# Ten products of the identity ahead of the first data, and a new order of the first loads, in a two-layer mixture and adapter kernel

## The chip, the cores and the metric

The kernel runs on one NeuronCore of a Trainium2 chip. The metric is device time in microseconds (us), the median of several runs. The engines are named as in the profile: PE is TensorE (the matmul array) and PEld its weight loads, DVE is VectorE, ACT is ScalarE, POOL is GpSimd, and SP is SyncE, which here only issues DMA transfers (loads and stores). "SPq" and "ACTq" are the instruction queues from which those engines issue transfers.

## The reference

The input `x` has 8 sequences of 256 tokens with 1024 features. Two residual layers follow. The first is a dense product with a mixture of low-rank experts, the second a dense product with one weight matrix per sequence, chosen by an id:

```python
base = jnp.einsum('btd,od->bto', x, W)
logits = jnp.einsum('btd,ed->bte', x, Wr) + one_hot(language_ids, 8)[:, None, :] * 5.0
topw, topi = jax.lax.top_k(logits, 2)
weights = jax.nn.softmax(topw, axis=-1)
gates = jnp.sum(one_hot(topi, 8) * weights[..., None], axis=-2)
h = jnp.einsum('btd,erd->bter', x, A)                  # 8 experts of rank 16
lora_out = jnp.einsum('bter,bte,eor->bto', h, gates, B)
x = x + base + 2.0 * lora_out
x = x + jnp.einsum('bsi,boi->bso', x, weight[adapter_ids])
```

`W`, and each `weight[i]`, is 1024 by 1024. `A` gives 128 columns per feature and `Wr` gives 8. All numbers are float32.

## The kernel before, in words

The host lays out `x` as blocks: `xT[i, j, c]` is feature half `i`, token half `j` (1024 tokens) and half `c` of that token half (512 tokens). Such a chunk holds four pieces `k` of 128 features by 512 tokens, 256 KB each. The blocks live in SBUF as `xb["11"]` to `xb["22"]`, where the profile calls them `x`. `A` and `Wr`, transposed and joined, are `aw_sb`: for each of the eight 128-feature pieces, 136 columns, 68 KB. It lies in the memory of a `y` block, so the profile calls it `y`.

The head of the kernel issues all loads of the first layer. `load_x` (line 104) and `load_w` (line 109) issue from SyncE. `load_aw` (line 112) issues from ScalarE in three pieces, of two, two and four feature pieces (lines 115, 118 and 119). The language and adapter ids, 8 integers each, copied to all 128 partitions, follow on ScalarE (lines 122 and 123). On SyncE come the four 256 KB pieces of `xT[0, 0, 0]` one by one (line 117), the two 512 KB halves of `xT[1, 0, 0]` (lines 120 and 121), and then whole 1 MB chunks of x, the four blocks of W and B.

The tile framework gives each load one of eight DMA semaphores in turn, counted over both issuing engines, so that a load waits at its issue until the load eight before it has landed. The order of loads in the source is therefore also the order of these waits.

GpSimd meanwhile makes `ident`, a 128 by 128 identity matrix, and two small index tables.

From line 510 on, the order of instructions is the one written out by hand. `use_ids()` (line 151) turns the ids into a bias table and adapter numbers, in small VectorE operations. `project(j, c)` (line 186) computes `h` and the logits for 512 tokens: for each of eight feature pieces and four groups of 128 tokens it multiplies an x tile (128 by 128, the weights of the array) with a piece of `aw_sb` (136 columns), adding up in the PSUM tile `ps_h`. So the first quarter, `project(0, 0)`, needs all of `aw_sb` and the chunks `xT[0, 0, 0]` and `xT[1, 0, 0]`; `project(0, 1)` needs `xT[0, 0, 1]` and `xT[1, 0, 1]`, and so on for the four quarters. After each quarter VectorE adds the bias and writes the logits `lg`, and ScalarE copies `h` out. `gating(j)` turns logits into gates for a token half, and `turn(j)` transposes the gated `h` with products of `ident` into `ps_g`.

Then come the seven products of a Strassen scheme for the first layer (`product`, line 356; PSUM tiles A, B and X at line 366), with sums and differences of blocks made by VectorE between them, and 16 groups of the second layer (`adapter_group`, line 462; products at line 474), each half of the output columns of one sequence. The adapter weights are loaded by SyncE from `load_w1` (line 417), three groups ahead. All PSUM tiles come from one pool of four (`bank`, line 87) and go round in order.

Of the kernel before, what the change touches and what calls it, by code (L numbers as in the profile page):

```python
# [16 lines left out]
P = 128  # L17
NE = 8
LANG_BIAS = 5.0
SCALING = 2.0  # L20
NEG = -3.0e38


@with_exitstack
def kernel(
# [25 lines left out]
    nc = tc.nc  # L51
# [9 lines left out]
    KH = KC // 2  # L61
# [22 lines left out]
    def flat(blk):  # L84
        return blk.rearrange("p k n -> p (k n)")

    def bank(name):
        return psum.tile([P, 2, TQ], F32, name=name, tag="acc")
# [10 lines left out]
    aw_sb = flat(yb["12"])[:, : KC * EA].rearrange("p (k e) -> p k e", k=KC)  # L99
    hT = [flat(yb["22"])[:, j * C * ER : (j + 1) * C * ER].rearrange("p (c e) -> p c e", c=C) for j in range(2)]  # L100
    b_sb = const.tile([ER, O], F32, name="b_sb")
    ids = const.tile([P, 2, NB], I32, name="ids")

    def load_x(queue, i, j, c, k0, k1):
        queue.dma_start(  # L105
            xb[f"{i+1}{j+1}"][:, k0:k1, c * TQ : (c + 1) * TQ], xT[i, j, c, :, k0:k1, :]
        )
# [1 line left out]
    def load_w(i, j):  # L109
        nc.sync.dma_start(wb[f"{i+1}{j+1}"], wT[i, j])  # L110

    def load_aw(k0, k1):
        nc.scalar.dma_start(aw_sb[:, k0:k1, :], awT[:, k0:k1, :])  # L113

    load_aw(0, 2)
    for k in range(KH):
        load_x(nc.sync, 0, 0, 0, k, k + 1)
    load_aw(2, 4)
    load_aw(4, 8)
    load_x(nc.sync, 1, 0, 0, 0, 2)  # L120
    load_x(nc.sync, 1, 0, 0, 2, 4)
    nc.scalar.dma_start(ids[:, 0, :], lang.partition_broadcast(P))
    nc.scalar.dma_start(ids[:, 1, :], adapt.partition_broadcast(P))
    load_x(nc.sync, 0, 0, 1, 0, 4)
    load_x(nc.sync, 1, 0, 1, 0, 4)
    load_x(nc.sync, 0, 1, 0, 0, 4)
# [10 lines left out]
    ident = const.tile([P, P], F32, name="ident")  # L137
# [13 lines left out]
    def use_ids():  # L151
        nc.vector.tensor_copy(ids_f, ids)

        nc.vector.tensor_tensor(
            bias,
            ids_f[:, 0, :].unsqueeze(2).to_broadcast([P, NB, E]),
            ecol.unsqueeze(1).to_broadcast([P, NB, E]),
            ALU.is_equal,
        )
        nc.vector.tensor_scalar(bias, bias, LANG_BIAS, None, ALU.mult)  # L160

        wrap = const.tile([P, NB], F32, name="wrap")
        nc.vector.tensor_scalar(wrap, ids_f[:, 1, :], 0.0, float(NAD), ALU.is_lt, ALU.mult)
        nc.vector.tensor_tensor(wrap, ids_f[:, 1, :], wrap, ALU.add)
        nc.vector.tensor_scalar(aid_i, wrap, 0.0, float(NAD - 1), ALU.max, ALU.min)
# [20 lines left out]
    def project(j, c):  # L186

        ps = bank(f"ps_h_{j}_{c}")
        for k in range(KC):
            for r in range(CQ):  # L190
                v, u = divmod(r, 2)
                nc.tensor.matmul(  # L192
                    ps[:, v, u * EA : (u + 1) * EA],
                    lhsT=xk(k, j, c)[:, ts(r, P)],
                    rhs=aw_sb[:, k, :],
                    start=(k == 0 and u == 0),
                    stop=(k == KC - 1),
                    skip_group_check=True,
                )
        ps = ps[:, :, : 2 * EA].rearrange("p v (u e) -> p v u e", u=2)  # L200
        split = lambda t: t[:, c * CQ : (c + 1) * CQ, :].rearrange("p (v u) e -> p v u e", v=2)
        nb = CQ * P // S
        b0 = (2 * j + c) * nb
        add(
            split(lg[j]),
            ps[:, :, :, ER:],
            bias[:, b0 : b0 + nb, :].unsqueeze(2).to_broadcast([P, nb, CQ // nb, E]),
        )
        nc.scalar.copy(split(hT[j]), ps[:, :, :, :ER])
# [16 lines left out]
    def gating(j):  # L226
# [11 lines left out]
        def onto_h():  # L238
# [5 lines left out]
        ops = ops1 + [  # L244
            lambda: nc.vector.scalar_tensor_tensor(rest, hot1, NEG, lg[j], ALU.mult, ALU.add)
        ] + ops2 + [
# [261 lines left out]


    ctx.enter_context(tc.manual_schedule())  # L510
    use_ids()
    project(0, 0)
    project(0, 1)
# [104 lines left out]
```

## Time and profile before

| what | us |
|---|---|
| median of 3 runs (lowest to highest) | 434.15 (434.06 to 434.67) |
| the profiled execution | 434.59 |
| its span, from first to last instruction | 432.8 |
| PE busy in the span | 422.8 |
| DVE busy in the span | 273.7 |
| first product of `project` starts at | 5.35 |
| last product of `project` ends at about | 38.5 |

The profile is of one execution; times in it count from the start of the span. A line of a group or a wait names the source line, the engine, the operation and the tiles, `out<-in`. A wait is put down to what ended it. A stage table gives, for a stretch of time, the busy time of each engine with the number of its instructions, the granted clock of TensorE, the mean busy share of the core's 16 DMA engines, and the GB/s that they moved. A float32 product shows as two records of PE.

### The profile page before, as it was taken

The page shows a single profiled execution, that of the slowest core. Times are in us where ns is not written, and L with a number is a line of the kernel's source. Part 1 is how long each engine was busy: PE and PEld are TensorE (multiplying, and loading weights), DVE is VectorE, ACT ScalarE, POOL GpSimd, SP SyncE. Part 2 cuts the span into 40 slices and gives each one's busy share as a digit, 9 for nine tenths or more (in the row PEclk, how much of TensorE's full clock was granted, in tenths as well). Part 3 has the DMA queues.
Part 4 walks back from the last instruction along what each step waited for, and adds up shares of the span by engine and source line. Part 5 has one row for each costly group of instructions (what it writes and reads, how often), then busy time and mean ns, then how long its engine had stood idle before and what let it go on. Part 6 is the DMA issues. An engine that isn't in the chain of part 4 may idle for free.

```text
span 432.8 us, 4177 instructions
## 1 busy us (share of the span) xinstructions
PE 422.8 (98%) x1624; PEld 289.8 (67%) x1624; DVE 273.7 (63%) x347; ACT 37.8 (9%) x81; POOL 0.9 (0%) x8
## 2 busy tenths in 40 slices
PE   5899999999999999999999999999999999999996
PEld 4897444444444444444445888888888888888885
DVE  1058696744538887999864756666776656666631
ACT  1011210002000000000000111111111111111110
POOL 0000000000000000000000000000000000000000
PEclk9999999999999999999999999999999999999999
DMA  7996000000002020045000056655555555665211
GB/s 221 391 402 253 0 0 2 0 0 0 2 0 97 8 89 0 2 165 220 3 0 0 26 220 243 242 228 192 192 195 221 219 231 224 243 242 203 89 48 50
DMA packets 14963, 55.88 MB, mean 129 GB/s; under 512 B 1632, under 2 KB 1888, under 8 KB 10336
## 3 DMA queue, kind: packets, MB, share of 16 engines
q1 hardware_dynamic: 14224, 55.06, 33.8%
q10 hardware_dynamic: 720, 0.57, 0.4%
q8 instruction: 13, 0.21, 0.2%
q14 instruction: 6, 0.05, 0.0%
HBM read 47.23 MB, written 8.39 MB: 128 GB/s over the span
## 4 chain that ended last, share of the span: by engine, by line
PE 96%; DMA 3%; ACTq 0%; SPq 0%; ACT 0%; issue 0%
PE A L474 26%; PE A L366 24%; PE B L366 14%; PE B L474 13%; PE X L366 7%; PE X L474 6%; PE ps_h L192 5%; DMA x<-xT_dram 2%; DMA y<-awT_dram 1%; PE ps_g L263 0%; ACTq L113 0%; SPq L105 0%; ACT w L352 0%; ACTq L352 0%
## 5 line engine op out<-in xcount | busy, mean ns | idle before, releaser
L366 PE MATMUL A<-t,s 128*128 128x512 f32 x112 | 50.4, 592 | 0.0
L474 PE MATMUL B<-x,w 128*128 128x256 f32 x192 | 45.4, 379 | 0.0
L168 DVE TENSOR_TENSOR w<-X,w 128x256 f32<-128x256 f32 x16 | 6.8, 425 | 59.9 <-PE X L474 59.9
L474 PE MATMUL A<-x,y 128*128 128x256 f32 x192 | 44.2, 379 | 0.0
L352 ACT COPY w<-A 128x256 f32<-128x256 f32 x48 | 17.9, 372 | 257.2 <-PE A L474 257.2
L474 PEld LDWEIGHTS A<-x,y 128*128 128x128 f32 x192 | 36.5, 190 | 5.4 <-issue 0.5
L474 PEld LDWEIGHTS B<-x,w 128*128 128x128 f32 x192 | 36.5, 190 | 5.0
L168 DVE TENSOR_TENSOR x<-x 128x1024 f32<-128x1024 f32 x32 | 39.1, 1222 | 0.8
L366 PEld LDWEIGHTS A<-t,s 128*128 128x128 f32 x112 | 21.3, 190 | 26.8 <-issue 26.8
L192 PE MATMUL ps_h<-y,x 128*128 128x136 f32 x256 | 32.0, 288 | 6.5 <-DMA y<-awT_dram 5.3
L168 DVE TENSOR_TENSOR y<-A,y 128x1024 f32<-128x1024 f32 x22 | 26.8, 1220 | 17.3 <-PE A L366 17.3
L192 PEld LDWEIGHTS ps_h<-y,x 128*128 128x128 f32 x256 | 31.3, 198 | 6.9 <-DMA y<-awT_dram 5.3
L474 PE MATMUL X<-x,y 128*128 128x256 f32 x128 | 30.2, 379 | 0.0
L168 DVE TENSOR_TENSOR x<-x,x 128x1024 f32<-128x1024 f32 x24 | 28.6, 1216 | 0.0
L474 PEld LDWEIGHTS X<-x,y 128*128 128x128 f32 x128 | 24.3, 190 | 3.3
L366 PE MATMUL A<-x,w 128*128 128x512 f32 x56 | 25.2, 592 | 0.0
L366 PE MATMUL B<-t,s 128*128 128x512 f32 x56 | 25.2, 592 | 0.0
L366 PE MATMUL X<-x,w 128*128 128x512 f32 x56 | 25.2, 592 | 0.0
L366 PE MATMUL B<-x,s 128*128 128x512 f32 x56 | 25.2, 592 | 0.0
L366 PE MATMUL A<-t,w 128*128 128x512 f32 x56 | 25.2, 592 | 0.0
L168 DVE TENSOR_TENSOR y<-B,y 128x1024 f32<-128x1024 f32 x12 | 14.6, 1221 | 16.2 <-PE B L366 16.2
L474 PE MATMUL A<-w,w 128*128 128x256 f32 x96 | 22.7, 379 | 0.0
(92 smaller groups left out, 433.5 us busy)
## 6 DMA issues: line engine op xcount, KB each, us to landing
x<-w_dram SPq DMA_DIRECT2D x32, 1024.0 KB, 5.0
out_dram<-w SPq DMA_DIRECT2D x32, 256.0 KB, 2.0
x<-xT_dram SPq DMA_DIRECT2D x6, 1024.0 KB, 13.3
w<-wT_dram SPq DMA_DIRECT2D x4, 1024.0 KB, 14.4
x<-xT_dram SPq DMA_DIRECT2D x4, 256.0 KB, 4.6
x<-xT_dram SPq DMA_DIRECT2D x2, 512.0 KB, 6.6
b_sb<-bT_dram SPq DMA_DIRECT2D x1, 512.0 KB, 14.7
y<-awT_dram ACTq DMA_DIRECT2D x2, 136.0 KB, 4.8
```

Of the source, the lines that this page charges most:

```text
L168: nc.vector.tensor_tensor(out_, x, y, op)
L192: nc.tensor.matmul(ps[:, v, u * EA : (u + 1) * EA], lhsT=xk(k, j, c)[:, ts(r, P)], rhs=aw_sb[:, k, :], start=(k == 0 and u == 0), stop=(k ...
L352: nc.scalar.copy(dest, acc)
L366: nc.tensor.matmul(acc[:, m, :], lhsT=l, rhs=r, start=(first and i < 2), stop=(i >= len(steps) - 2), skip_group_check=True,)
L474: nc.tensor.matmul(acc[name], lhsT=lhs[:, k // 2, k % 2, :], rhs=rhs[:, k, :], start=(first and k == 0), stop=(k == KH - 1), skip_group_ch ...
```

## The change

Three things change in the head, and nothing after it.

First, a PSUM tile `idle` is taken from the pool and ten products of `ident` with itself are written into it, ahead of the first `project`. Nothing reads the tile.

Second, `load_aw` takes its queue. ScalarE issues only the first piece of `aw_sb`; SyncE issues pieces 1 to 2 after the first 256 KB of x, and pieces 3 to 7 after the third.

Third, the loads of the ids move from ScalarE to SyncE, behind the two halves of `xT[1, 0, 0]` and ahead of the 1 MB chunk `xT[0, 0, 1]`.

```diff
+WARM = 10
...
-    def load_aw(k0, k1):
-        nc.scalar.dma_start(aw_sb[:, k0:k1, :], awT[:, k0:k1, :])
-
-    load_aw(0, 2)
-    for k in range(KH):
-        load_x(nc.sync, 0, 0, 0, k, k + 1)
-    load_aw(2, 4)
-    load_aw(4, 8)
+    def load_aw(queue, k0, k1):
+        queue.dma_start(aw_sb[:, k0:k1, :], awT[:, k0:k1, :])
+
+    load_aw(nc.scalar, 0, 1)
+    load_x(nc.sync, 0, 0, 0, 0, 1)
+    load_aw(nc.sync, 1, 3)
+    load_x(nc.sync, 0, 0, 0, 1, 2)
+    load_x(nc.sync, 0, 0, 0, 2, 3)
+    load_aw(nc.sync, 3, 8)
+    load_x(nc.sync, 0, 0, 0, 3, 4)
     load_x(nc.sync, 1, 0, 0, 0, 2)
     load_x(nc.sync, 1, 0, 0, 2, 4)
-    nc.scalar.dma_start(ids[:, 0, :], lang.partition_broadcast(P))
-    nc.scalar.dma_start(ids[:, 1, :], adapt.partition_broadcast(P))
+    nc.sync.dma_start(ids[:, 0, :], lang.partition_broadcast(P))
+    nc.sync.dma_start(ids[:, 1, :], adapt.partition_broadcast(P))
     load_x(nc.sync, 0, 0, 1, 0, 4)
...
     ctx.enter_context(tc.manual_schedule())
+
+    idle = bank("idle")
+    for i in range(WARM):
+        nc.tensor.matmul(idle[:, 0, :P], lhsT=ident, rhs=ident, start=True, stop=True)
     use_ids()
     project(0, 0)
```

## The prediction

> **What bounds the kernel now.** I read the page's engine lines first, then the waits of TensorE, then the chain for the first 45 us, then DMA rates by stage.
>
> ```profile
> span 432.8 us, 4177 instructions
> PE 422.8 (98%) x1624; PEld 289.8 (67%) x1624; DVE 273.7 (63%) x347; ACT 37.8 (9%) x81; POOL 0.9 (0%) x8
> PE ps_h L192 <- DMA y<-awT_dram: 5.3, 1, 5.3
> PE ps_h L192 <- DMA x<-xT_dram: 1.1, 1, 1.1
> ```
>
> TensorE is busy for 98%, and its two listed waits are both in the head: 5.3 us for the first piece of A and Wr (`aw`), and 1.1 us for an x chunk. The chain (start, duration, what) says where its freedom ends:
>
> ```profile
> 1.17 5.07 DMA y<-awT_dram
> ...
> 6.68 9.26 DMA x<-xT_dram
> 15.95 0.04 issue
> 15.99 22.51 PE ps_h L192 x192
> 38.50 0.87 PE ps_g L263 x8
> ```
>
> From 15.99 us TensorE runs without a stop to the end. What started it there is a transfer that landed at 15.95: the 1 MB chunk `x(0,0,1)`, needed by `project(0, 1)`, issued at 6.68. So the end moves only as far as this chunk does (with TensorE ready for it), or as far as TensorE work is added behind it. This transfer is one in a stream, so I read the stream: stage, length, busy time of each engine (count), granted clock, DMA share, GB/s.
>
> ```profile
> 4.00:6.00 2.00, 0.65 (x3) 0.65 (x4) 0.00 (x0) 0.64 (x1) 0.00 (x0) 1.00 0.99 355
> 6.00:7.50 1.50, 1.50 (x8) 1.50 (x8) 0.00 (x0) 0.00 (x0) 0.00 (x0) 1.00 0.72 242
> 7.50:9.50 2.00, 2.00 (x16) 2.00 (x14) 1.16 (x8) 0.00 (x0) 0.00 (x0) 1.00 1.03 272
> 9.50:11.50 2.00, 1.32 (x12) 1.12 (x10) 0.00 (x0) 0.00 (x0) 0.00 (x0) 1.00 0.94 334
> 11.50:15.50 4.00, 3.57 (x30) 3.58 (x31) 0.00 (x0) 0.00 (x0) 0.00 (x0) 1.00 1.05 400
> 15.50:37.00 21.50, 21.41 (x185) 21.21 (x184) 11.19 (x30) 1.96 (x4) 0.00 (x0) 1.00 1.04 402
> ```
>
> The stream holds 400 GB/s from 11.5 us on, but dips between 6 and 11.5. SyncE's own waits say why:
>
> ```profile
> SPq L105 <- DMA y<-awT_dram: 3.4, 2, 3.2
> ```
>
> After three x loads SyncE sits 3.2 us until the first `aw` lands, and can only then issue the fourth. That issue is at 5.32 and lands 4.2 us later; so a hole opens at about 6.5.
>
> The cold array is the other cost of the head (TensorE columns are busy time and count):
>
> ```profile
> 5.35:8.30 2.95, 2.95 (x13) 2.95 (x14) 0.00 (x0) 0.00 (x0) 1.00 0.86 291
> 11.93:15.75 3.82, 3.82 (x32) 3.77 (x32) 0.00 (x0) 0.00 (x0) 1.00 1.05 399
> ```
>
> A product is two passes here (128 products in `project`, 256 records). At first a pass takes 2.95/13 = 0.227 us, later 3.71/32 = 0.116 us[...]. The granted clock column says 1.00 in both and doesn't show this.
>
> **The skill.** "TensorE: Matmul & The Clock Gate", Part 1, What's actually happening: the array starts at half clock and is released after about 3.4 us of sustained work. The trace agrees in kind: half rate for 2.9 us after the first product, then full. The same page, HAM oscillation, says idle gaps over some 3.4 us bring the slow state back; the 1.1 us wait here did not. "DMA: Bandwidth & Descriptors", Issuing engines are not separate DMA queues: loads of SyncE and ScalarE share the same DMA engines, and a second issuer saves only issue time. The trace agrees: SyncE's queue alone moves 400 GB/s. So moving `aw` and the ids to SyncE costs no bandwidth as such.
>
> **The change part by part.**
>
> *Order of loads.* As the changed kernel is built, DMA semaphores go round in eight, and a load waits for the one eight before it. Before, the eight were 3 x, 3 `aw` and 2 ids (4 KB each), so SyncE's fourth x load waited for the first `aw`. Now the first eight are `aw`(0), x0, `aw`(1-2), x1, x2, `aw`(3-7), x3 and the half chunk x(1,0,0) 0:2, and none waits. At 0.42 us per issue (the three `aw` issues take 1.38), SyncE's seven are out by 0.74 + 7 x 0.42 = 3.7 us, 2.1 MB together. The next, half chunk 2:4, waits for `aw`(0), which lands by about 5.0. The 1 MB chunk waits for x1 (about 6.5), its data then starting about 2 us later, at 8.5. By then the stream still has the half chunks to move (until 10.0, below). So no hole.
>
> Saved at 400 GB/s: 1.5 x (1 - 242/400) = 0.59, 2.0 x (1 - 272/400) = 0.64, 2.0 x (1 - 334/400) = 0.33, sum 1.56 us. Bounds: 0.59 if the slow packets of 7.5 to 11.5 come from the small chunks themselves, 1.56 if they are the restart after the hole. I take the restart: in 4.0 to 6.0 the same quarter chunks moved at 355, and from 1.5 to 4.0, the other start of a stream, only at 139.
>
> *The ids* now go in SyncE's stream ahead of the 1 MB chunk: 256 packets of 32 bytes. Before, they landed at 7.7 and 7.9 in the hole, 0.2 us apart, so they cost nothing there. Now I charge 0.3 us for both (0.1 to 0.5). Behind them on SyncE, the next loads wait for x1 and x2, which land near the same time: no new delay. Their reader, VectorE's eight small operations (8.05 to 9.3 before), runs about 12 to 13 us, before the first quarter ends. If later, only `lg` and the eviction of `ps_h` would wait; the cover is the time until `turn(0)` reads the gated result at 38.2, with gating done at 29.7 now.
>
> *Start of the stream.* The bytes ahead of the first product fall from 256 + 136 KB to 256 + 68 KB, but the stream from 1.5 to 6.0 carries the same requests: gain to the 1 MB chunk 0 (bounds -0.5 if one queue starts more slowly than two, +0.9 if the deeper queue fills half of the 1.76 us lost between 1.5 and 4.5, where 129 and 201 GB/s moved).
>
> Net on the 1 MB chunk: 1.56 - 0.3 = 1.26 us, landing 15.95 to 14.7. A check by bytes: 1.06 MB are moved by 6.0 (139 x 2.5 + 355 x 2.0); through the chunk it is 3.71 MB, so 6.0 + 2.65/0.400 + 0.3 = 12.9, and transfers landed about 1.75 us after that count (before: count reached at 14.2, landed 15.95): 14.7 again.
>
> *The ten products.* 20 passes, no data but `ident`, which GpSimd ends at 1.35. Cold a pass of 128 columns takes 0.227 x 128/136 = 0.213. From 1.45: fourteen cold passes to about 4.4, six at 0.11 to 5.1; all cold, to 5.7. The first real product could start about 5.0, so 5.1 to 5.2. Then all 64 passes of the quarter run at 0.116.
>
> *Is TensorE ready at 14.7?* A k piece is 8 passes, 0.93 us. With cumulative bytes and the lag above (1.3 to 1.75): k0 at 5.2; x1 lands 6.5, k1 to 7.4; k2 to 8.4; x3 lands 8.9, k3 to 9.8; half chunk 0:2 lands 10.4, two pieces to 12.3; the rest to 14.1. Ready, 0.6 us early. Without the warm passes, 12 more cold ones (12 x 0.111 = 1.3 us at k0 and k1) would be mostly absorbed by the waits at k3 and k4. So the ten products earn about nothing; the queue earns it all.
>
> *After it* everything moves together: SyncE's order from the 1 MB chunk on is the old one, and it is already saturated. The next chunk landed at 18.7 where TensorE wanted it at 15.99 + 32 x 0.116 = 19.7: 1.0 us spare, kept. PSUM tiles rotate over four; `idle` only shifts which bank each gets. The last waits of VectorE and ScalarE are on TensorE.
>
> Sum: span 432.8 - 1.26 = 431.5. The profiled execution took 434.59, 1.8 more than its span; that overhead stays. The median of the runs is 434.15, so 432.9.
>
> **Rivals.**
> *Only the hole closes* (slow small chunks): for it, the DMA share is 1.03 while only 272 GB/s move, so the engines weren't short of requests; against it, 355 for the same shapes. Gain 0.59 - 0.3 = 0.3, up to 0.8 if half the slow packets vanish: 433.35 to 433.85, within the noise.
> *The start fills as well*: eight loads queued at once raise the 1.5 to 4.5 rate, +0.9: gain 2.15, time 432.0. There the quarter's 64 passes (5.0 + 7.4 = 12.4 at best) just keep up, and the warm passes do earn. Against: issue wasn't the limit there.
> *The little packets stall the ring*: the ids, between the half chunk and the 1 MB chunk, take more than they leave. 16 packets on each of 16 engines; they turn the gain at 1.56 us (0.1 us per packet) and make the kernel slower by 0.9 at 2.4 us (0.15 per packet): 435.0. Against: 0.2 us for each id load before, though with little beside them.
> *The change does nothing*, the array being the bound: not so, since TensorE starts at a landing.
>
> **How the numbers follow.** The likeliest case (0.55): 432.9, its own range 432.3 to 433.25. Fuller start: 0.13. Only the hole: 0.25. Stalled ring or another loss: 0.07. About 0.2% (0.87 us) is what a measurement of this kernel can tell from no change; so faster 0.68, same 0.25, slower 0.07. The range runs from the fuller start's far side, 431.5, to the upper end of the hole-only case, 434.0.
>
> **What would show it.** After: SyncE without the 3.2 us wait; DMA at 355 to 400 from 4 us on, with no dip to 242; the 1 MB chunk landing near 14.7 and TensorE unbroken from there; 0.116 us passes from the first real product; waits of a few tenths inside the quarter; ids' VectorE work near 12. Wrong if the dip stays (small chunks are slow), if the ids open a dip of their own near 10, or if TensorE's unbroken run starts at a product that was not waiting for data.

## The result and the profile after

The changed kernel took 438.08 us (median of 6 runs, 435.70 to 438.88) against 434.35 us for the kernel before on the same occasions. The ratio is 1.0076, with a 95% interval of 1.006 to 1.0091. It is slower by 3.7 us, where 432.9 us had been forecast, and the stated range ended at 434.0. Five of the six runs took 437.69 us or more, at a mean clock of 0.991 to 0.996; the sixth took 435.70 at 1.0.

The profiled execution took 438.03 us and its span is 436.3 us, 3.5 us more than before. The chain for the first 45 us (start, duration, what) shows where TensorE's unbroken run starts now:

```profile
6.29 11.44 DMA x<-xT_dram
17.72 0.04 issue
17.77 24.18 PE ps_h L195 x192
41.94 0.87 PE ps_g L266 x8
```

Two things went wrong. The 1 MB chunk that starts the run lands at 17.72 instead of 15.95, so the run starts 1.78 us later. And its 192 passes of `project` take 24.18 us instead of 22.51, which is 1.67 us more. The sum is 3.45 us, the whole loss in the span.

The stages show the first of the two (stage, length, busy time of PE, PEld, DVE, ACT and POOL, granted clock, DMA share, GB/s):

```profile
4.00:6.00 2.00, 2.00 (x14) 2.00 (x14) 0.00 (x0) 0.00 (x0) 0.00 (x0) 1.00 1.00 332
6.00:7.50 1.50, 1.50 (x16) 1.49 (x14) 0.00 (x0) 0.00 (x0) 0.00 (x0) 1.00 1.02 314
7.50:9.50 2.00, 1.59 (x13) 1.42 (x12) 0.00 (x0) 0.00 (x0) 0.00 (x0) 1.00 1.04 389
9.50:11.50 2.00, 1.93 (x17) 1.72 (x16) 0.00 (x0) 0.00 (x0) 0.00 (x0) 1.00 0.76 216
11.50:15.50 4.00, 2.79 (x25) 2.59 (x23) 0.40 (x2) 0.00 (x0) 0.00 (x0) 1.00 0.80 307
```

The old dip is gone: 314 and 389 GB/s stand where 242 and 272 stood. A new and larger one opens at 9.5 us, where the loads of the ids come up. The DMA engines are idle for a part of it: their share falls from 1.04 to 0.76. The rate falls further, from 389 to 216 GB/s, so what they move there moves more slowly, too. These two loads of 4 KB, issued at 5.15 and 5.74, land 9.4 and 9.2 us later, at about 14.5 and 15.0; before, they landed 5.6 and 5.3 us after their issue. VectorE's work on the ids starts at 15.1 instead of 12, but no wait of TensorE is put down to it.

Then TensorE's rows in order of time (start, duration, operation, count, idle time before it):

```profile
1.41 4.39 PE L517 MATMUL idle<-ident 128*128 128x128 f32 x20 [1.41 <-POOL ident masks.py:199]
5.64 3.02 PE L195 MATMUL ps_h<-y,x 128*128 128x136 f32 x24
9.08 5.21 PE L195 MATMUL ps_h<-y,x 128*128 128x136 f32 x40 [0.41 <-DMA x<-xT_dram]
17.77 2.55 PE L195 MATMUL ps_h<-y,x 128*128 128x136 f32 x15 [3.48 <-DMA x<-xT_dram]
```

And the stages behind its long wait, where the clock is the number ahead of the DMA share:

```profile
17.77:19.00 1.23, 1.23 (x10) 1.23 (x11) 0.00 (x0) 0.00 (x0) 0.00 (x0) 1.00 1.05 388
19.00:22.40 3.40, 3.40 (x18) 3.40 (x17) 0.00 (x0) 0.00 (x0) 0.00 (x0) 0.51 1.07 396
22.40:25.00 2.60, 2.60 (x24) 2.60 (x24) 0.00 (x0) 0.00 (x0) 0.00 (x0) 0.98 1.00 392
```

The first quarter is done at 14.3, as forecast (14.1). Then the array idles for 3.48 us, runs on at full clock for 1.2 us, and from 19.0 to 22.4 at half clock. Here the clock column shows it (0.51); at the start of the run it says 1.00 over passes at half rate.

### The profile page after: what moved, and what is told of

Same layout as the page of the kernel before. It is cut to its first block, busy times and chain, and to the rows that moved or that the text cites. A ratio compares the mean times of both kernels' runs of the same rounds, so it can differ in the third digit from the quotient of the medians.

```text
span 436.3 us, 4217 instructions
## 1 busy us (share of the span) xinstructions
PE 427.4 (98%) x1644; PEld 294.2 (67%) x1644; DVE 273.9 (63%) x347; ACT 37.8 (9%) x81; POOL 0.9 (0%) x8
## 4 chain that ended last, share of the span: by engine, by line
PE 95%; DMA 4%; SPq 0%; ACT 0%; issue 0%; ACTq 0%
PE A L477 25%; PE A L369 24%; PE B L369 14%; PE B L477 13%; PE X L369 7%; PE X L477 6%; PE ps_h L195 6%; DMA x<-xT_dram 3%; DMA y<-awT_dram 1%; PE ps_g L266 0%; SPq L125 0%; SPq L126 0%; SPq L106 0%; ACT w L355 0%; ACTq L355 0%
## 5 line engine op out<-in xcount | busy, mean ns | idle before, releaser
L171 DVE TENSOR_TENSOR y<-B,y 128x1024 f32<-128x1024 f32 x12 | 14.7, 1223 | 16.2 <-PE B L369 16.2
## 6 DMA issues: line engine op xcount, KB each, us to landing
x<-xT_dram SPq DMA_DIRECT2D x6, 1024.0 KB, 14.5
```

What stands on the lines that cost most here:

```text
L171: nc.vector.tensor_tensor(out_, x, y, op)
```

## The experiments

The kernel before took 434.51 to 434.57 us beside the first fifteen experiments and 434.37 us beside the last; ratios are against these. "The chunk" is the 1 MB chunk `xT[0, 0, 1]`. The theory was that the ids' small packets hold up a full stream, and that the wait which follows cools the array.

**The ids back on ScalarE.** The rest of the change is kept.

```diff
-    nc.sync.dma_start(ids[:, 0, :], lang.partition_broadcast(P))
-    nc.sync.dma_start(ids[:, 1, :], adapt.partition_broadcast(P))
+    nc.scalar.dma_start(ids[:, 0, :], lang.partition_broadcast(P))
+    nc.scalar.dma_start(ids[:, 1, :], adapt.partition_broadcast(P))
```

> The changed kernel with the two loads of the ids back on ScalarE, where they are issued right after its piece of A and Wr. Theory (the ids' 256 small packets, queued in SyncE's full stream, hold the stream up by 1.9 us, and the wait of 3.5 us that follows cools the array, 1.7 us more): no dip from 9.5 to 14.5 us, the 1 MB chunk lands at 14.5 to 15.2, no slow passes after it, 432.7 to 433.4. Rival 1 (the pieces of A and Wr between the chunks are the cause): the chunk still lands near 17.7, 436 to 438. Rival 2 (small packets hold up a full stream on whichever queue they come): the dip moves to 5 to 9 us, the chunk lands at 16.5 or later, 435 to 438.

434.55 us, ratio 1.000 (0.9991 to 1.0008), above what the theory expected. On ScalarE they are issued right after its piece of `aw`, at 1.2 and 1.7 us, and the dip moves to 4 to 7.5 us:

```profile
1.50:4.00 2.50, 2.50 (x12) 2.50 (x13) 0.00 (x0) 1.28 (x1) 0.00 (x0) 1.00 0.69 169
4.00:6.00 2.00, 2.00 (x15) 2.00 (x15) 0.00 (x0) 0.00 (x0) 0.00 (x0) 1.00 0.73 142
6.00:7.50 1.50, 0.59 (x6) 0.39 (x4) 0.00 (x0) 0.00 (x0) 0.00 (x0) 1.00 0.58 180
```

The edit does more than its lines say. With the ids among ScalarE's first loads, SyncE's fourth x load is the ninth in turn, as in the kernel before, and SyncE waits again:

```profile
SPq L106 <- DMA y<-awT_dram: 1.9, 1, 1.9
SPq L106 <- DMA ids<-adapt_dram: 1.0, 1, 1.0
```

That wait alone doesn't explain the dip. By 3.0 us three x pieces and all of `aw` had been issued, 1.34 MB, and by 7.5 us only some 0.98 MB had moved (an estimate from the stage rates). So the stream was slow while loads were queued, and the dip has come with the ids to the other queue: it isn't bound to SyncE's. How much of the late landing at 15.57 is the dip and how much the old wait, this run doesn't tell. The pieces of `aw` between the chunks are cleared: with them the chunk lands at 15.57, not near 17.7. This is the second rival in kind, though not in size.

**Without the ten products** (the five lines around `idle` are left out).

> The changed kernel without the ten products; the order of loads as in the changed kernel. Theory (the products end the first quarter early and so lengthen the wait for the 1 MB chunk to 3.5 us, after which the array runs at half clock): the chunk still lands near 17.7, but the wait before it is 2.0 to 2.6 us, no slow passes follow, 435.8 to 436.4. Rival 1 (the slow passes come of something else, a limit on power): 437.7 to 438.3. Rival 2 (the products are worth their 1.3 us at the end of the first quarter): slower than the changed kernel, over 438.5.

438.25 us (436.34 to 439.80), ratio 1.0097 (1.0078 to 1.0116). The theory fell for this run. Its profiled execution, the fastest, has no slow passes and a span of 434.6; its wait was 3.0 us, longer than the 2.0 to 2.6 expected. But the other three took 438.2 or more at a mean clock of 0.991 to 0.996. So slow passes come without the products, too. How long the array waited in those three isn't known, as there is no trace of them.

**The ids on ScalarE and no products.**

> The changed kernel with the ids on ScalarE and without the products: what the order of the other loads is worth alone. Theory (the order earns 1.3 us by closing the hole, the products nothing, since the 1 MB chunk ends the quarter): 432.7 to 433.4, the same as with the products within 0.3. Rival 1 (the products earn, as the quarter is bound by the array once the loads flow): 0.5 to 1.5 us slower than with the products. Rival 2 (the small chunks are slow in themselves, the order is worth nothing): 434.0 to 434.5.

435.66 us, ratio 1.0027 (1.0017 to 1.0036), 1.1 us slower than with the products: rival 1. With the ids early, and SyncE waiting for `aw` again (1.8 us), x pieces land late, and the profile has the first quarter's products unbroken from 8.56, at half clock until about 12 (15 passes in 3.44 us). There the array, not the chunk, ends the quarter, and the products are worth their price.

**The ten products alone**, in the kernel before.

> The kernel before with the ten products alone. Theory (in the kernel before the first quarter waits for loads twice and the 1 MB chunk ends it, so the products earn nothing): 434.0 to 434.5. The wait at the half chunk grows from 1.1 to about 2.3 us, which leaves the array warm. Rival 1 (they save the 1.3 us of slow passes): 432.8 to 433.3. Rival 2 (they do harm on their own, by a longer wait that cools the array): 435 to 436.

434.69 us, ratio 1.0002 (0.9993 to 1.0011): nothing, as the theory had it. The profiled execution happened to be the slowest of 12 (435.90; the others took 434.31 to 434.94). In it, after waits of 0.4 and 1.7 us with 8 passes between them, the array ran at half clock:

```profile
11.93:15.50 3.57, 3.57 (x16) 3.57 (x17) 0.00 (x0) 0.00 (x0) 0.00 (x0) 0.52 1.05 400
```

So waits shorter than 3 us, close together, can do it too.

**The ids from rows of their own.** The host repeats each list of ids 128 times, and each partition reads its own row. Packets, their size, place and queue stay.

```diff
-    nc.sync.dma_start(ids[:, 0, :], lang.partition_broadcast(P))
-    nc.sync.dma_start(ids[:, 1, :], adapt.partition_broadcast(P))
+    nc.sync.dma_start(ids[:, 0, :], lang)
+    nc.sync.dma_start(ids[:, 1, :], adapt)
...
-        "lang": np.asarray(itok_B_0_7).reshape(1, NB),
+        "lang": np.repeat(np.asarray(itok_B_0_7).reshape(1, NB), P, 0),
```

> The changed kernel, but the ids are laid out on the host in 128 equal rows, and each partition reads a row of its own: the same 256 packets of 32 bytes in the same place of the same queue, only their source addresses differ. Theory (reading one address 256 times is what holds the stream up): no dip from 9.5 to 14.5 us, the 1 MB chunk lands at 14.1 to 14.9, no slow passes after it, 432.3 to 433.1. Rival (small packets as such, or their place in the queue): the dip stays, the chunk lands at 17 or later, 435.5 to 438.5.

433.14 us (433.07 to 433.22), ratio 0.9967 (0.9954 to 0.9979). The dip is gone and the chunk lands at 14.41, as the stages and then the chain show:

```profile
1.50:4.00 2.50, 2.50 (x12) 2.50 (x13) 0.15 (x1) 0.95 (x1) 0.00 (x0) 1.00 0.71 164
4.00:6.00 2.00, 2.00 (x11) 2.00 (x11) 0.00 (x0) 0.00 (x0) 0.00 (x0) 1.00 0.99 343
6.00:7.50 1.50, 1.50 (x14) 1.50 (x13) 0.00 (x0) 0.00 (x0) 0.00 (x0) 1.00 0.98 337
7.50:9.50 2.00, 2.00 (x18) 1.92 (x18) 0.00 (x0) 0.00 (x0) 0.00 (x0) 1.00 1.03 381
9.50:11.50 2.00, 1.90 (x16) 1.70 (x16) 0.00 (x0) 0.00 (x0) 0.00 (x0) 1.00 1.08 362
11.50:15.50 4.00, 3.69 (x32) 3.49 (x32) 1.20 (x7) 0.59 (x1) 0.00 (x0) 1.00 1.05 394
```

```profile
7.06 7.35 DMA x<-xT_dram
14.41 0.04 issue
14.45 22.51 PE ps_h L195 x192
```

Neither the size of the packets nor their place in the queue is enough to cause the dip. It takes packets that read one address. In the changed kernel this cost the chunk 17.72 - 14.41 = 3.3 us.

**The ids two chunks later**, from one address as they were.

> The changed kernel with the two loads of the ids, as they were, moved two 1 MB chunks further back on SyncE, behind the first chunk of the third quarter. Theory (the ids' loads hold up the stream wherever they stand, and it is the place that hurts): the 1 MB chunk lands at 14.1 to 14.9, a dip of about 1.9 us comes at 17 to 22 us instead and eats the spare time of the chunks behind it, with a wait of at most 0.6 us there: 432.5 to 433.5. Rival 1 (the ids are innocent and the order of the other loads is slow): 436 to 438. Rival 2 (the dip costs its full length later): 434.2 to 435.

433.23 us, ratio 0.9971 (0.9958 to 0.9983). The chunk lands at 14.21, and the delay comes further back in the stream: a wait of 0.9 us ahead of the last quarter, more than the 0.6 that was expected. Most of the delay falls into time that the later chunks have to spare.

**The kernel before, ids from rows.**

> The kernel before with the ids read from 128 rows, all else as it was: SyncE's wait for the first piece of A and Wr stays. Theory (part of the dip of 6 to 9.5 us in the kernel before, which the prediction gave to that wait, was the ids' loads too): the dip shrinks, the 1 MB chunk lands at 14.4 to 15.3 instead of 15.95, 432.7 to 433.5. Rival (the dip is the hole that the wait leaves): nothing moves, 434.2 to 434.8.

434.32 us, ratio 0.9994 (0.9985 to 1.0002): the theory fell, the rival holds. The dip only moves a little later (339 GB/s in 6.0 to 7.5, then 292 and 262 up to 11.5). SyncE's wait for `aw` is still there, and the dip of the kernel before is what this wait leaves, as the prediction said: it stays when the ids change, and goes when the order does. The ids cost next to nothing in it.

**Ids from rows, no products.**

> As the changed kernel with ids in 128 rows, and without the ten products: what the products are worth once the loads flow. Theory (the first quarter without them ends at about 14.7, as it did when the ids held up only what came after it, against a chunk that lands at 14.1 to 14.9): 0.2 to 0.7 us slower than with them. Rival 1 (nothing at all, the chunk decides): within 0.15. Rival 2 (the full 1.3 us of slow passes): 1.1 to 1.5 slower.

433.02 us (432.99 to 433.12), ratio 0.9963 (0.9949 to 0.9978), 0.12 us less than with the products: rival 1, they are worth nothing here. TensorE's first real product starts at 4.83 in place of 5.84, which makes up for most of the slow passes: the quarter ends at 14.29 against 14.14, ahead of the chunk either way (14.49 and 14.41).

**The long wait filled** with fourteen more products of `ident` between the first two quarters; loads as in the changed kernel.

```diff
     project(0, 0)
+    fill = bank("fill")
+    for i in range(14):
+        nc.tensor.matmul(fill[:, 0, :P], lhsT=ident, rhs=ident, start=True, stop=True)
     project(0, 1)
```

> The changed kernel with fourteen more products of the identity (28 passes, 3.0 us) between the first and the second quarter, where the array waits 3.5 us for the 1 MB chunk; all loads as in the changed kernel. Theory (2 us of the changed kernel's loss come of the array going to half clock in that wait): the chunk lands near 17.7 as before, no slow passes follow, 435.6 to 436.5, and the runs lie closer together. Rival (the slow passes have another cause, or the products only delay the second quarter): 437.5 or more.

436.23 us (435.89 to 437.27), ratio 1.0045 (1.0031 to 1.006), about 1.9 us below the changed kernel. The chunk is as late as before, but the passes behind it are fast, 22.51 us for 192 instead of 24.18:

```profile
14.27 3.29 PE L522 MATMUL fill<-ident 128*128 128x128 f32 x28
17.61 22.51 PE L195 MATMUL ps_h<-y,x 128*128 128x136 f32 x192
```

So the slow passes come of the idle array. This is the second part of the loss, shown by itself.

**One list from one address, the other from rows**, once each way.

> The changed kernel with the language ids read from 128 rows and the adapter ids from one address, as they were. Theory (each read of one address adds its own delay): half the dip, about 0.9 us, the 1 MB chunk at 15.0 to 16.2, 433.6 to 435. Rival 1 (the delay is there as soon as one such load is in the stream): the chunk at 17 or later, 435.5 to 438.5. Rival 2 (it takes two such loads against each other): 433.0 to 433.3.

> The counterpart of the run with one of the two: here the language ids are read from one address and the adapter ids from 128 rows. Theory (one load from one address passes in a full stream, it takes two of them): no dip, the 1 MB chunk at 14.1 to 14.9, 432.7 to 433.4. Rival (it is this load, the first, that holds the stream up, and the adapter ids were innocent): dip and chunk as in the changed kernel, 17 or later, 435.5 to 438.5.

433.02 us, ratio 0.9965 (0.9953 to 0.9978), with the adapter ids from one address; 433.19 us, ratio 0.9984 (0.9958 to 1.001), with the language ids so (six runs from 433.05 to 433.24 and one of 437.03). Both profiles are without a dip. Here the stage from 9.5 to 14.5 us of four kernels, in this order: the changed kernel, ids from rows, adapter ids from one address, language ids from one address.

```profile
9.50:14.50 5.00, 4.72 (x39) 4.31 (x37) 0.00 (x0) 0.00 (x0) 0.00 (x0) 1.00 0.74 251
```

```profile
9.50:14.50 5.00, 4.59 (x38) 4.19 (x37) 1.20 (x7) 0.09 (x1) 0.00 (x0) 1.00 1.06 383
```

```profile
9.50:14.50 5.00, 4.69 (x38) 4.28 (x37) 1.21 (x7) 0.14 (x1) 0.00 (x0) 1.00 1.06 383
```

```profile
9.50:14.50 5.00, 4.71 (x39) 4.31 (x37) 1.17 (x7) 0.00 (x0) 0.00 (x0) 1.00 1.06 386
```

The delay isn't the sum of two halves. In these profiles one load from one address passed freely, whichever it was, and the two in a row did not. Of the rivals stated, this is that it takes two. What has to be two stays open: two such loads are also 256 reads of this kind close together in place of 128, and no run tried one load with 256. The run of 437.03, at a mean clock of 0.995, has no trace; a single load may not be quite safe.

**Two rows of 512 bytes.** Ids from rows, and behind them two loads that nothing uses, each of one 512-byte row into all partitions.

```diff
+    for i in range(2):
+        nc.sync.dma_start(row[:, i, :], xT[0, 0, 0, i : i + 1, 0, :P].partition_broadcast(P))
```

> The changed kernel with the ids read from 128 rows, and behind them two loads that nothing uses: one row of 512 bytes each, read from one address into all 128 partitions, 0.13 MB in all. By bytes at 400 GB/s they cost 0.33 us. Theory (the delay is per read of one address, whatever its length): a dip like that of the ids, the 1 MB chunk at 16 or later, over 434.5. Rival (it is the reads of 32 bytes that queue up at one place, and 512 bytes are spread over more of the memory): the chunk at 14.6 to 15.2, 433.3 to 433.8.

437.79 us, ratio 1.0076 (1.0059 to 1.0093), chunk at 17.73. By bytes 0.33 us had been due. The chunk was issued 1.0 us later than with ids from rows alone (8.08 against 7.06), which can't make up the 3.3 us. So the delay isn't peculiar to the ids' tensors or to 32 bytes. The DMA share stays at 1.03 here while the rate falls, so idle engines aren't what all such dips have in common:

```profile
9.50:14.50 5.00, 4.72 (x39) 4.32 (x37) 1.18 (x7) 0.00 (x0) 0.00 (x0) 1.00 1.03 263
```

**The two lists apart**, 2 MB of x between them.

> The changed kernel with both ids read from one address each, as they were, but 2 MB of x between the two loads. Theory (the two hold the stream up only when their reads meet): no dip, the 1 MB chunk at 14.1 to 14.9, no wait behind it, 432.7 to 433.4. Rival 1 (the first load alone holds the stream up): chunk at 17 or later, over 435.5. Rival 2 (any two such loads near each other, the second one pays): chunk at 14.9 or earlier, but a dip of 1.9 us from 15 to 20 us, which the third quarter's chunk pays, 433.5 to 435.

433.18 us, ratio 0.9976 (0.9969 to 0.9983). The profile has no dip and the chunk at 14.29, as the theory had it. But the 20 runs go from 432.88 to 434.89, where the six with ids from rows stayed within 0.15.

**One packed load.** The two lists lie side by side in one tensor, and one load from one address brings both, 64 bytes per partition; first without the products, then with them. The third way is to load the lists into one partition and spread them with a product of ones between the first two quarters, no ten products.

```diff
-    nc.sync.dma_start(ids[:, 0, :], lang.partition_broadcast(P))
-    nc.sync.dma_start(ids[:, 1, :], adapt.partition_broadcast(P))
+    nc.sync.dma_start(ids, lang.partition_broadcast(P))
```

> The order of loads of the changed kernel without the ten products, and the two lists of ids side by side in one tensor, read by one load from one address into 128 partitions, 64 bytes each. Theory (one such load passes freely): 1 MB chunk at 14.1 to 14.9, 432.7 to 433.4, as with ids in 128 rows. Rival (one load of this kind suffices): chunk at 16 or later, over 434.5.

> The changed kernel with all its parts, the ten products too, and the two lists of ids read by one load in place of two. Theory (with the products the first quarter is ready before the 1 MB chunk lands, without them it is late by up to 0.6 us in some runs): 432.8 to 433.2, runs within 0.5 us of each other, against 433.62 and 433.07 to 434.68 without the products. Rival (the products are worth nothing, the spread without them has another cause): 433.5 or more, with the same spread.

> A version that keeps the inputs as they were: the order of loads of the changed kernel, no ten products, each of the two id lists read once into one partition, and spread to 128 partitions by a product with a row of ones between the first and the second quarter, copied out by VectorE. Theory (two packets in place of 256 leave the stream alone, the product hides in the wait of 0.25 us for the 1 MB chunk or adds its 0.1 to 0.3 us): chunk at 14.1 to 14.9, 432.7 to 433.4. Rival (a load into one partition is itself slow to land, or the array waits for VectorE): 434 or more.

Packed: 433.62 us (433.07 to 434.68), ratio 0.9984 (0.9975 to 0.9993). Packed with products: 433.38 us (432.64 to 434.99), ratio 0.9982 (0.9974 to 0.999). The spread is no smaller with the products, so its cause isn't the cold start; whether the 0.24 us are theirs can't be told. Spread by a product: 433.74 us (432.94 to 435.00), ratio 0.9982 (0.9973 to 0.9991); the first quarter ended at 14.8, after the chunk, and the product of ones came on top (0.39 us in its row). This kernel has no load from one address into all partitions, and its runs spread as far, so the spread can't be put down to such loads alone. All three beat both kernels a little; ids from rows of their own beat both by more, and with the closest runs.

## Why the prediction was wrong

**The step that failed is the price of the ids in SyncE's stream.** It charged 0.3 us for both loads (0.1 to 0.5), from their landing 0.2 us apart in the kernel before. There they had fallen into the hole, where the stream moved 242 GB/s, and the run with ids from rows in the kernel before shows that they cost next to nothing in that place. In a full stream (389 GB/s just ahead of them) the same packets cost the chunk 3.3 us, ten times the charge. The rival of the stalled ring named the place, gave it too small a chance, and took the small packets for the reason. What the runs show instead is that two loads in a row each read one address for all partitions: the same packets in the same place, reading other addresses, let the chunk land at 14.41.

**A second step was missing**: what is late next when a stall goes beyond the forecast. The section of the Trainium skill that the prediction cited ("TensorE: Matmul & The Clock Gate", HAM oscillation) puts the limit at idle gaps of some 3.4 us, and the wait came to 3.48. The rival of the stalled ring was priced at 435.0 without the slow passes. Filling the wait took about 1.9 us off again; the profile puts the slow passes at 1.67 us. The page's limit isn't sharp here: in the kernel before with the products, half clock followed waits of 0.4 and 1.7 us in the profiled run. And without the products three of four runs show a mean clock of 0.991 to 0.996, though the one with a profile, where the wait was 3.0 us, doesn't.

**The order of loads was right.** SyncE's 3.2 us wait is gone; the longest wait of its kind is 0.7 us in the changed kernel (total, count, longest):

```profile
SPq L106 <- DMA y<-awT_dram: 1.0, 2, 0.7
```

The chunk was to land at 14.7 and lands at 14.41 once the ids are out of the way. 433.14 and 433.02 us stand against 432.9. The term for the hole (1.56 us) came out, too: less the 0.3 for the ids it gave 1.26, and the kernel with ids from rows gained 434.55 - 433.14 = 1.41. Part of this is luck. From 4.0 to 7.5 us that stream moved 343 and 337 GB/s, where 355 to 400 were expected, so 3.71 MB were moved by about 13.1 us instead of 12.9 (an estimate from the stage rates). The landing then followed 1.3 us later, where 1.75 had been assumed.

**The ten products earn nothing**: right, 434.69 against 434.56 alone and 433.14 against 433.02 with loads that flow. With the ids on ScalarE, where the first pieces landed late, they earned 1.1 us. One number was off. In the changed kernel eighteen passes were cold instead of fourteen, so the first real product started at 5.64 instead of 5.1 to 5.2, after its data had landed at 4.7. The later waits took that up.

**TensorE's end follows the chunk**: right in each run with an early first quarter. All that follows the chunk moved as one block, in passes of 22.51/192 = 0.117 us, close to the 0.116 assumed. The kernel with the ids two chunks later adds its wait of 0.9 us behind that.

## What to carry to other kernels

That a small load costs nothing in a gap of the stream says nothing about its price in a full one; give it the stage's whole traffic when it is moved. Don't put two loads that broadcast one row to all partitions one behind the other into a stream that something waits for: let partitions read rows of their own, keep them apart, or place them where later transfers have time to spare. And when a wait grows to about 3 us, add the passes at half clock that may follow it: they cost 1.67 us here.

## What the runs showed of the hardware

- Two loads in a row, each from one address into 128 partitions (4 KB each), held a stream of some 385 GB/s down to 251 for 5 us and a transfer behind them up by 3.3 us. The DMA share fell from 1.06 to 0.74. With 512 bytes a row the rate fell as far (263), at a share of 1.03. A dip came with the two loads on ScalarE's queue, too (142 and 180 GB/s), but there no run read other addresses beside it. Why it takes two, whether loads or reads are what counts, and what in the memory or the DMA engines waits, no run shows. A single such load passed in every profile.
- The bytes lost, 5.0 x (1 - 251/383) = 1.7 us, are fewer than the chunk's delay of 3.3 us. That the DMA engines which weren't held up went on with the chunks behind would explain it; this is argued, not shown.
- The slow passes last 3.4 us, but don't always begin with the end of the wait: in the changed kernel 1.2 us after it (17.77 to 19.0), with two rows of 512 bytes 0.5 us after it (17.77 to 18.3), and in the kernel before with the products at once (11.93).
